# Two-layer cross-attention on one core: the sums of the second layer's softmax are formed by DMA, GpSimd and VectorE in place of TensorE

## The chip, the cores and the metric

The kernel runs on one core of a Trainium2 chip. The metric is the device time of one execution in microseconds (us). Before the change it is 2887.03 us, the median of three runs (2881.52 to 2888.2).

## What is computed

The input is a batch of four sequences, `x` (4 x 1024 x 512) and a context (4 x 1024 x 384), in f32. Two cross-attention layers follow one another; only the second is touched. Cut to what matters:

```python
# layer 0: layernorm, 16 heads of 64, softmax over 1024 keys, projection, x = x + out
# layer 1:
xn = x * rsqrt(mean(x * x) + 1e-5) * norm_w
q = rotate(xn @ wq), k = rotate(ctx @ wk)          # 16 heads of 32
q, k = q / |q|, k / |k|
attn = softmax(q @ k.T * sqrt(32), over 1024 keys)
x = x + (attn @ v) @ wout
```

Since the rows of q and k have length 1, no maximum is subtracted in layer 1: the exponentials are taken of the scores as they are, `attn @ v` is formed with the unnormalized exponentials, and the result is divided by their sum over the keys.

## The kernel before, in words

The four batches are done one after the other. For each, layer 0 is a stage of some 500 us and layer 1 one of some 240 us. The order of all instructions is the order in which the program issues them (L120, a hand-made schedule); each engine, and the SP queue that issues nearly all DMAs, works through its own list in that order and stops at an instruction until everything that it waits for is there.

**Layer 1.** Its 16 heads are done in two halves of eight heads; a half holds two groups `g` of four heads (four heads of 32 rows fill 128 partitions). The 1024 queries are cut into four parts `qb` of `WQ` = 256. A block is one `(qb, g)`, so a half has eight blocks (loop at L911). A block has four steps `kk` over the keys, 256 keys each; a half has 32 steps (one call of `Attention1.step`, L574, each), and the whole kernel has 64 blocks and 256 steps.

One step does this:

- TensorE: eight score products (L586), keys on the partitions and queries along the row.
- ScalarE: two exponentials of 128x1024 (L596) into `e`, which has two buffers that alternate with `kk`.
- TensorE: the product with v of the step before (L635), into the PSUM tile `av`.
- `self.u.fill(us)`: a share of other work ("units") that is waiting. In half 0 these are the projections and rotations of q and k for the second half and the values; in half 1 they are the first output projection of layer 1 (`po`, with weights `wo1` loaded by `wo_load`, L682, called at L892) and the start of the next batch: its loads (context rows L183, rows of x L274, weights L308), its transposes and projections.
- VectorE: the exponentials are added up over the step's two chunks of 128 keys (L605) and over the steps (L607, and L609 at the block's end) into `both`. What is left is a sum over the 128 partitions.

**The sums over the partitions** are what the change is about. In 56 blocks (`lone`), `late` (L655) multiplies `both` by a matrix of ones on TensorE (L659: four calls, eight instructions, since an f32 product is done in two passes). It is put at the third step of the next block and goes into the free half of that block's `av`. ScalarE copies `av` and the sums out together (L647, 128x512), and VectorE takes a reciprocal of 128x256 (L652) and multiplies (L653). In the last eight blocks of the kernel (the last half of the last batch) `sums` (L668) does the same with eight calls (L671) and without the addition of L609.

**Buffers.** `both`, and a tile `rest` that holds the copies of `av`, an unused quarter and the values of half 1, have two slots of the pool `big`; layer 0 uses the same slots for its regrouped exponentials. Layer 0 already regroups by DMA: L413 issues 16 DMAs from 32 partitions to 32 others for each block, 2048 in all, on SP.

**The SP queue around layer 1.** Before the first half the weights of layer 1 are loaded. The program then issues no DMA until the second half, whose first are `wo1` (L892), the next batch's weights (L308) and context rows (L183).

Of the kernel before, what the change touches and what calls it, by code (L numbers as in the profile page):

```python
# [33 lines left out]
F32 = mybir.dt.float32  # L34
# [76 lines left out]
def xattn_kernel(ctx: ExitStack, tc: tile.TileContext, a: dict, out: bass.AP):  # L111
# [444 lines left out]
    class Attention1:  # L556


        def __init__(self, b, units):
            self.b, self.u = b, units  # L560
            self.last = None
            self.av = None
            self.sums = self.quotient = None
            self.late = self.beside = None
            self.lone = False
            self.n = 0
            self.e = sb.tile([P, 2, 2, 2, 2, WQ], F32, tag="e", bufs=2, name=f"e1_{b}")
            self.both = sb.tile([P, 4, 4, WQ], F32, tag="big", bufs=2, name=f"both_{b}")
            rest = sb.tile([P, 4, 1024], F32, tag="big", bufs=2, name=f"rest_{b}")
            self.avs = rest[:, 0].rearrange("p (n c q) -> p n c q", n=2, c=2)  # L570
            v1 = rest[:, 2:].rearrange("p g (t f) -> p g t f", f=P)
            self.v1 = [v1[:, g] for g in range(2)]

        def step(self, half, g, qb, kk, kT, qT, v, o, us):  # L574
            n = f"{self.b}_{half}_{g}_{qb}_{kk}"
            self.n += kk == 0
            if kk == 1:
                self.add_up()
            if kk == 2 and self.late is not None:
                self.late(False)  # L580
            sc = [score(f"s1_{n}_{u}", (P, 2, 2, WQ)) for u in range(2)]
# [16 lines left out]
            self.finish()  # L598
            self.last = (half, g, qb, kk, v, es, o, self.n % 2, self.lone)
            self.u.fill(us)  # L600
# [5 lines left out]
            if 0 < kk < NT // 2 - 1:  # L606
                nc.vector.tensor_add(acc, acc, into)  # L607
            if kk == NT // 2 - 1 and self.lone:
                nc.vector.tensor_add(acc, acc, end)  # L609

# [15 lines left out]
        def product(self):  # L626
            half, g, qb, kk, v, es, o, par, lone = self.last
            n = f"{self.b}_{half}_{g}_{qb}"
# [13 lines left out]
            if end:  # L642
                s, av = self.avs[:, par], self.av
                if self.beside is None:
                    nc.scalar.copy(s[:, 0, :], av[:, 0, :])
                else:
                    nc.scalar.copy(s, av)  # L647
                    self.quotient = lambda f=self.beside: f(s[:, 1, :])
                    self.beside = None

                def divide(by=s[:, 1, :]):
                    nc.vector.reciprocal(by, by)  # L652
                    nc.vector.tensor_mul(o[g][:, qb * WQ : (qb + 1) * WQ], s[:, 0, :], by)  # L653

                def late(alone):  # L655
                    to = (av if alone else self.av)[:, 1, :]
                    for j in range(4):
                        rr = slice(j * HD1, (j + 1) * HD1)
                        nc.tensor.matmul(to[rr], ones, self.both[:, par, j], start=alone, stop=alone)  # L659
                    self.late = None  # L660
                    if alone:
                        nc.scalar.copy(s[:, 1, :], to)
                        self.quotient = divide
                    else:
                        self.beside = divide

# [7 lines left out]

                if lone:
                    self.late = late
                else:
                    self.sums = sums
# [78 lines left out]
    for b in range(B):  # L757
# [115 lines left out]
        for half in range(2):  # L873
# [27 lines left out]
            final = b == B - 1 and half == 1  # L901
            att1.lone = not final
            if final:
# [6 lines left out]
                ]  # L910
            for qb, g in blocks:  # L911
                for kk in range(NT // 2):
# [9 lines left out]
            kT, qT, v = kT1, qT1, att1.v1  # L922
        att1.finish()
        if att1.late is not None:
            att1.quotient()
            att1.late(True)
        att1.add_up()
# [47 lines left out]
```

## Time and profile before

| | |
|---|---|
| median of three runs | 2887.03 us |
| span of the profiled execution | 2885.9 us |
| mean granted TensorE clock | 0.996 |
| layer 1, half 0 of batch 1 (1214 to 1340 us): busy | PE 122.3, DVE 109.4, ACT 83.3, POOL 50.0 of 126 us |
| layer 1, half 1 of batch 1 (1340 to 1460 us): busy | PE 119.7, DVE 101.5, ACT 78.5, POOL 3.1 of 120 us |
| DMA engines, share busy in these two | 0.06 and 0.12 |

PE is TensorE, DVE VectorE, ACT ScalarE, POOL GpSimd, and SPq the queue of DMA issues on SyncE. The span is from the first to the last instruction; it lies 1.1 us under the median, so that times worked out from the trace can be set against the median as they are. The profile's groups give, for each line and shape, the count, the busy time in all, the mean of one, and the idle time of the engine ahead of them with what ended it.

### The profile page before, as it was taken

The numbers are of one execution on the slowest core, as the hardware profiler recorded it, in microseconds if no ns is written. First come the engines' busy times: TensorE is split into PE (matmuls) and PEld (weight loads), VectorE is DVE, ScalarE is ACT, GpSimd is POOL, SyncE is SP. The second block draws the span as 40 slices with busy tenths as digits, with TensorE's granted clock in tenths as the row PEclk, the third lists the DMA queues.
The fourth block names the chain that finished last, engine by engine and source line by source line (L and its number), as shares of the span: only waits on it lengthen the run. The fifth ranks groups of instructions, "written<-read, shape, count | busy, mean of one in ns | idle before, by whom it ended". The sixth has DMA issues, their size and how long they took to land.

```text
span 2885.9 us, 65749 instructions
## 1 busy us (share of the span) xinstructions
PE 2827.9 (98%) x26888; PEld 1420.5 (49%) x26888; DVE 2248.4 (78%) x3008; ACT 1430.1 (50%) x2276; POOL 947.8 (33%) x776
## 2 busy tenths in 40 slices
PE   8999999999999999999999999999999999999998
PEld 4444445555444445555544445455554444445543
DVE  5677786898777778589877777959987777785987
ACT  4443443666444444466643444446664444444664
POOL 2343344320134335342023433534202333353410
PEclk9999999999999999999999999999999999999999
DMA  5887776010298777501039887740105887773000
GB/s 138 183 188 176 174 170 150 22 37 25 73 207 189 180 173 174 128 22 36 26 93 205 195 184 165 178 103 22 37 26 121 203 196 184 163 173 83 2 2 31
DMA packets 177549, 348.81 MB, mean 121 GB/s; under 512 B 37600, under 2 KB 93152, under 8 KB 177248
## 3 DMA queue, kind: packets, MB, share of 16 engines
q1 hardware_dynamic: 175920, 343.96, 50.9%
q8 instruction: 212, 3.47, 0.5%
q14 instruction: 89, 0.73, 0.1%
q10 hardware_dynamic: 1328, 0.66, 0.1%
HBM read 67.64 MB, written 8.39 MB: 26 GB/s over the span
## 4 chain that ended last, share of the span: by engine, by line
PE 87%; DVE 3%; SPq 3%; DMA 2%; ACT 2%; issue 1%; POOL 1%; ACTq 0%; DVEq 0%
PE s L368 16%; PE av L429 14%; PE po L166 11%; PE s L586 9%; PE av L635 8%; PE pv L166 7%; PE pqT L166 7%; PE pkT L166 5%; PE q_p L166 4%; PE k_p L166 3%; SPq L413 2%; DMA eT<-e 1%; ACT e L596 1%; PE av L659 1%; DVE m L393 1%
## 5 line engine op out<-in xcount | busy, mean ns | idle before, releaser
L393 DVE TENSOR_REDUCE m<-s 128x1 f32<-128x1024 f32 x512 | 602.9, 1219 | 381.5 <-PE s L368 380.9
L596 ACT ACTIVATE e<-s 128x1024 f32<-128x1024 f32 x512 | 496.5, 1022 | 295.3 <-PE s L586 288.9
L399 POOL TENSOR_SCALAR raw<-raw,li 128x1024 f32<-128x1024 f32 x256 | 286.1, 1118 | 734.1 <-DVE li L398 725.6
L368 PE MATMUL s<-qk 64*128 64x512 f32 x2048 | 519.1, 616 | 3.0 <-ACT e L394 2.2
L394 ACT ACTIVATE e<-s,m 128x1024 f32<-128x1024 f32 x256 | 282.8, 1109 | 465.2 <-DVE m L393 224.3
L394 ACT ACTIVATE raw<-s,m 128x1024 f32<-128x1024 f32 x256 | 285.1, 1114 | 458.7 <-DVE m L393 458.7
L429 PE MATMUL av<-eT,v 128*64 128x256 f32 x4096 | 472.8, 384 | 12.2 <-DMA eT<-e 9.1
L399 POOL TENSOR_SCALAR e<-e,li 128x1024 f32<-128x1024 f32 x256 | 286.1, 1118 | 472.6 <-DVE li L398 240.3
L429 PEld LDWEIGHTS av<-eT,v 128*64 128x64 f32 x4096 | 288.2, 137 | 232.1 <-issue 94.8
L605 DVE TENSOR_TENSOR both<-e 128x512 f32<-128x512 f32 x512 | 342.8, 702 | 64.3 <-ACT e L596 62.2
L368 PEld LDWEIGHTS s<-qk 64*128 64x128 f32 x2048 | 184.8, 186 | 285.2 <-issue 168.8
L586 PE MATMUL s<-q,k 32*128 32x256 f32 x4096 | 308.0, 402 | 5.3 <-ACT q L505 2.7
L402 DVE STREAM_TRANSPOSE e<-raw 128x1024 f32<-128x1024 f32 x256 | 309.9, 1228 | 1.7 <-DMA eT<-e 1.7
L402 DVE STREAM_TRANSPOSE e<-e 128x1024 f32<-128x1024 f32 x256 | 310.0, 1229 | 0.2
L586 PEld LDWEIGHTS s<-q,k 32*128 32x128 f32 x4096 | 193.9, 185 | 142.5 <-ACT e L596 66.4
L166 PE MATMUL pqT<-hT,w 128*64 128x512 f32 (+1 forms) x1216 | 241.9, 597 | 2.5 <-ACT hT L250 2.5
L166 PE MATMUL po<-wo,vals 128*64 128x512 f32 x1024 | 234.6, 596 | 0.0
L166 PEld LDWEIGHTS pv<-w,cT 128*64 128x64 f32 (+1 forms) x3360 | 170.4, 132 | 41.8 <-issue 34.1
L296 DVE TENSOR_TENSOR x<-x,po 128x512 f32<-128x512 f32 x200 | 131.7, 678 | 70.4 <-PE po L166 69.7
L166 PE MATMUL pv<-w,cT 128*64 128x128 f32 (+1 forms) x3360 | 184.3, 274 | 0.9 <-ACT hT L250 0.7
L166 PE MATMUL pkT<-cT,w 128*64 128x512 f32 (+1 forms) x912 | 182.0, 597 | 0.0
L607 DVE TENSOR_TENSOR both<-both 128x1024 f32<-128x1024 f32 x128 | 159.7, 1248 | 4.4
(87 smaller groups left out, 2801.3 us busy)
## 6 DMA issues: line engine op xcount, KB each, us to landing
eT<-e SPq DMA_DIRECT2D x2048, 128.0 KB, 2.4
xr<-in_x_dram SPq DMA_DIRECT2D x32, 256.0 KB, 4.0
wo<-in_Wo_dram SPq DMA_DIRECT2D x16, 512.0 KB, 3.9
x<-in_x_dram SPq DMA_DIRECT2D x32, 256.0 KB, 5.0
out_dram<-x SPq DMA_DIRECT2D x32, 256.0 KB, 2.7
w<-in_Wq_dram SPq DMA_DIRECT2D x31, 256.0 KB, 3.3
c<-in_ctx_dram SPq DMA_DIRECT2D x32, 192.0 KB, 3.9
wkv<-in_wkv_dram SPq DMA_DIRECT2D x16, 384.0 KB, 3.3
```

Of the source, the lines that this page charges most:

```text
L166: nc.tensor.matmul(o[rr], lhsT[:, rr], rhs, start=start, stop=stop)
L368: nc.tensor.matmul(sc[j][:, kb * 512 : (kb + 1) * 512], pr["qT"][r[j], i * P : (i + 1) * P], pr["kT"][r[j], kb * 512 : (kb + 1) * 512], st ...
L393: nc.vector.tensor_reduce(m[:, j : j + 1], sc[j], AX.X, ALU.max, negate=True)
L394: nc.scalar.activation(e[j], sc[j].rearrange("p (g s) -> p g s", g=4), AF.Exp, bias=m[:, j : j + 1], accum_out=l[:, j : j + 1])
L399: nc.gpsimd.tensor_scalar(e[j], e[j], li[:, j : j + 1], HD0**-0.5, ALU.mult, ALU.mult)
L402: self.turn = [lambda j=j: nc.vector.transpose(self.e[:, :, i % BQ * 2 + j, :], e[j]) for j in range(2)]
L429: nc.tensor.matmul(av[r[j], :W].rearrange("p (t a i) -> p t a i", t=BQ, a=4), pr["v"][:, k, r[j]], eT[:, j, :, :, k * 32 : (k + 1) * 32], ...
L586: nc.tensor.matmul(sc[j // 2][:, j % 2, c, :], kT[rr, g, k * P : (k + 1) * P], qT[rr, g, qb * WQ : (qb + 1) * WQ], start=True, stop=True,)
L596: nc.scalar.activation(e, sc[u], AF.Exp, scale=float(np.sqrt(np.float32(HD1))))
L605: nc.vector.tensor_add(into[:, 2 * u : 2 * u + 2, :], es[u][:, :, 0, :], es[u][:, :, 1, :])
L607: nc.vector.tensor_add(acc, acc, into)
L635: nc.tensor.matmul(self.av[rr, 0, :], v[g][:, 2 * kk + c, rr], es[j // 2][:, j % 2, c, :], start=first and c == 0, stop=end and c == 1,)
```

## The change

In 56 blocks the ones on TensorE go. At a block's end `regroup` issues 16 DMAs on SP, each a 32x256 piece (32 KB) of `both`, so that the four quarters of the partitions lie beside one another along the row in `parts` (a free quarter of `rest`). At the last step of the next block, `over` has GpSimd add the four quarters (128x512, then 128x256). At the first step of the block after that, `done` has VectorE turn 32x32 blocks, reduce 128x256 to 128x8, take the reciprocal of 128x8, turn it back spread over 32, and multiply. The division comes a block later than it did. ScalarE copies only the 128x256 of `av`.

`way` says which block does what: "regroup" for all but the last block of half 1 in the first three batches ("one": ones on TensorE after the half's end, as at a half's end before), and in the last half of the last batch "regroup" for the first three blocks and "two" (L671's way) for the last five.

```diff
-            if kk == 2 and self.late is not None:
-                self.late(False)
...
-            if kk == NT // 2 - 1 and self.lone:
-                nc.vector.tensor_add(acc, acc, end)
+            if kk == NT // 2 - 1:
+                if self.way != "two":
+                    nc.vector.tensor_add(acc, acc, end)
+                self.over()
+                if self.way == "regroup":
+                    self.regroup(self.n % 2, g, qb, o)
+            if kk == 0:
+                self.done()
+
+        def regroup(self, par, g, qb, o):
+
+            for a in range(4):
+                for j in range(4):
+                    nc.sync.dma_start(
+                        self.parts[j * HD1 : (j + 1) * HD1, a], self.both[a * HD1 : (a + 1) * HD1, par, j]
+                    )
+            s = self.avs[:, par]
+
+            def spread():
+                t, by = self.parts, s[:, 1, :]
+                nc.gpsimd.tensor_add(t[:, :2], t[:, :2], t[:, 2:])
+                nc.gpsimd.tensor_add(by, t[:, 0], t[:, 1])
+                self.turn = turn
+
+            def turn():
+                by = s[:, 1, :]
+                l = sb.tile([P, WQ // HD1], F32, tag="l1", bufs=1, name=f"l1_{self.b}_{self.n}")
+                nc.vector.transpose(by, by)
+                nc.vector.tensor_reduce(l, by.rearrange("p (c i) -> p c i", i=HD1), AX.X, ALU.add)
+                nc.vector.reciprocal(l, l)
+                nc.vector.transpose(
+                    by.rearrange("p (c i) -> p c i", i=HD1), l.unsqueeze(2).to_broadcast([P, WQ // HD1, HD1])
+                )
+                nc.vector.tensor_mul(o[g][:, qb * WQ : (qb + 1) * WQ], s[:, 0, :], by)
+
+            self.spread = spread
+
+        def over(self):
+            if self.spread is not None:
+                self.spread()
+                self.spread = None
+
+        def done(self):
+            if self.turn is not None:
+                self.turn()
+                self.turn = None
...
-                if self.beside is None:
-                    nc.scalar.copy(s[:, 0, :], av[:, 0, :])
-                else:
-                    nc.scalar.copy(s, av)
-                    self.quotient = lambda f=self.beside: f(s[:, 1, :])
-                    self.beside = None
+                nc.scalar.copy(s[:, 0, :], av[:, 0, :])
...
-            for qb, g in blocks:
+            for i, (qb, g) in enumerate(blocks):
+                att1.way = "two" if final and i > 2 else "one" if half == 1 and i == 7 else "regroup"
...
         att1.finish()
+        att1.done()
         if att1.late is not None:
-            att1.quotient()
-            att1.late(True)
+            att1.late()
```

More of the change, by code (lines that the diff above doesn't have):

```diff
@@ L563, in __init__ @@
             self.sums = self.quotient = None
-            self.late = self.beside = None
-            self.lone = False
+            self.late = None
+            self.way = "regroup"
             self.n = 0
@@ L570, in __init__ @@
             self.avs = rest[:, 0].rearrange("p (n c q) -> p n c q", n=2, c=2)
+            self.parts = rest[:, 1].rearrange("p (a q) -> p a q", q=WQ)
+            self.spread = self.turn = None
             v1 = rest[:, 2:].rearrange("p g (t f) -> p g t f", f=P)
@@ L598, in step @@
             self.finish()
-            self.last = (half, g, qb, kk, v, es, o, self.n % 2, self.lone)
+            self.last = (half, g, qb, kk, v, es, o, self.n % 2, self.way)
             self.u.fill(us)
@@ L626, in product @@
         def product(self):
-            half, g, qb, kk, v, es, o, par, lone = self.last
+            half, g, qb, kk, v, es, o, par, way = self.last
             n = f"{self.b}_{half}_{g}_{qb}"
@@ L643, in product, with divide, late @@
                 s, av = self.avs[:, par], self.av
-                if self.beside is None:
-                    nc.scalar.copy(s[:, 0, :], av[:, 0, :])
-                else:
-                    nc.scalar.copy(s, av)
-                    self.quotient = lambda f=self.beside: f(s[:, 1, :])
-                    self.beside = None
-                def divide(by=s[:, 1, :]):
+                nc.scalar.copy(s[:, 0, :], av[:, 0, :])
+                def divide():
+                    by = s[:, 1, :]
                     nc.vector.reciprocal(by, by)
                     nc.vector.tensor_mul(o[g][:, qb * WQ : (qb + 1) * WQ], s[:, 0, :], by)
-                def late(alone):
-                    to = (av if alone else self.av)[:, 1, :]
+                def late():
+                    to = av[:, 1, :]
                     for j in range(4):
                         rr = slice(j * HD1, (j + 1) * HD1)
-                        nc.tensor.matmul(to[rr], ones, self.both[:, par, j], start=alone, stop=alone)
+                        nc.tensor.matmul(to[rr], ones, self.both[:, par, j], start=True, stop=True)
                     self.late = None
[L661 to L665, printed above, removed]
+                    nc.scalar.copy(s[:, 1, :], to)
+                    self.quotient = divide
                 def sums():
@@ L673, in sums @@
                     self.quotient = divide
-                if lone:
+                if way == "one":
                     self.late = late
-                else:
+                elif way == "two":
                     self.sums = sums
@@ L901, in xattn_kernel @@
             final = b == B - 1 and half == 1
-            att1.lone = not final
             if final:
```

## The prediction, made before the changed kernel was run

> **What bounds the kernel.** I read the busy shares first, then the groups, then the order of time around layer 1.
>
> ```profile
> PE 2827.9 (98%) x26888; PEld 1420.5 (49%) x26888; DVE 2248.4 (78%) x3008; ACT 1430.1 (50%) x2276; POOL 947.8 (33%) x776
> ```
>
> TensorE is busy nearly always, and the chain of work that ended last gives it 87%. In layer 1 it is the same: PE fills 120 of 120 us in half 1 of batch 1. So each TensorE instruction taken out there shortens the run, as long as nothing else becomes late. The nearest to that is VectorE: in the second part of half 0 of batch 0 (567 to 629 us) PE has 62.0 us busy and DVE 58.7. From the groups, shapes kept apart:
>
> ```profile
> L652 DVE RECIPROCAL rest<-rest 128x256 f32<-128x256 f32 x64 | 111.8, 1746 | 7.8 <-ACT rest L672 5.3 <-ACT rest L662 1.5 <-ACT rest L647 0.9
> L653 DVE TENSOR_TENSOR o<-rest 128x256 f32<-128x256 f32 x64 | 27.2, 425 | 2.2
> L659 PE MATMUL av<-both,ones 128*32 128x256 f32 x448 | 34.6, 380 | 2.1 <-ACT rest L647 2.1
> ```
>
> Third, TensorE in order of time (start, length, what), where one set of ones stands:
>
> ```profile
> 601.12 1.48 PE L166 MATMUL q_p<-wq,hT 128*32 128x256 f32 x24
> 602.41 0.61 PE L659 MATMUL av<-both,ones 128*32 128x256 f32 x8
> 602.96 1.15 PE L586 MATMUL s<-q,k 32*128 32x256 f32 x16
> ```
>
> From one start to the next the ones take 0.55 us; the 0.61 includes an overlap.
>
> **What is saved.** The "one" way goes from 56 blocks to 3: 53 x 0.55 = 29.2 us. The "two" way goes from 8 to 5, each 16 instructions or 1.0 us: 3.0 us. Together 32.2 us of TensorE, if TensorE remains the bound everywhere.
>
> **VectorE and GpSimd.** Per block VectorE loses 1.75 + 0.425 = 2.17 us. It gets two turns (the row of 128x1024 takes 1.23, so a quarter is 0.31 to 0.43), a reduce (0.68 at 128x512, so 0.34 to 0.41), a short reciprocal (0.12 for 128x1) and the same multiplication (0.425): 1.5 to 1.8 us. It wins some 0.4 us a block. But GpSimd gets two additions (1.27 us for 128x512 at L285, half of that for 128x256: 1.9 us), and they get in VectorE's way, as one place shows:
>
> ```profile
> 606.71 1.37 POOL L492 TENSOR_TENSOR rot<-rot,q_r 128x512 f32<-128x512 f32 x1
> 607.20 1.95 DVE L607 TENSOR_TENSOR both<-both 128x1024 f32<-128x1024 f32 x1
> ```
>
> L607 usually takes 1.23; here it took 0.72 more and ended about 1.1 us after GpSimd did. So the price per block for VectorE is between 0 (GpSimd yields) and 1.9 us. There is also a wait: the turns wait for GpSimd, in whose list they may stand behind a rotation (0.6 + 3.2 + 1.6 us, L488, L170, L492). In the changed program's order one or two of the eight blocks of half 0 have a rotation in their last step. There VectorE has 3.8 us of work before the turn, against 5.4 + 1.9 = 7.3 us on GpSimd: a wait of up to 3.5 us, with all of VectorE's next additions behind it, and behind those the exponentials, since `e` has two buffers. Where VectorE has a fifth of its time free (first part of half 0, end of half 1) this costs nothing; in the four tightest blocks of each half 0 it eats the saving. I take off 16 x 0.55 = 9 us there and 5 us for the waits: of 32 us, 18 remain. Bounds: 32 (all hidden) and -8 (all locks and waits fall on the bound).
>
> ScalarE's copy falls from 0.59 to 0.37 us; it is half idle, so I count nothing.
>
> **The queue that is moved past.** This decides it. SP's issues around layer 1 of batch 0, before the change:
>
> ```profile
> 483.85 18.28 SPq L684 DMA_DIRECT2D wo<-in_wout_dram  x2
> 562.08 0.37 SPq L308 DMA_DIRECT2D w<-in_Wk_dram  x1
> ...
> 563.64 70.44 SPq L183 DMA_DIRECT2D c<-in_ctx_dram  x8
> 640.56 1.75 SPq L274 DMA_DIRECT2D xr<-in_x_dram  x4
> ```
>
> `wo1` (L684) stands in the program at the start of half 1, yet SP, which has nothing to do in half 0, issues it at 484 to 502 us; its first user runs at 627:
>
> ```profile
> 626.54 1.23 DVE L609 TENSOR_TENSOR both<-both 128x1024 f32<-128x1024 f32 x1
> 627.19 1.90 PE L166 MATMUL po<-wo,o 128*32 128x512 f32 x16
> ```
>
> In the changed program eight groups of 16 regroup DMAs of half 0 stand ahead of `wo1`. The last of them waits for L609's sum of the eighth block, which ends at 626.54 + 1.23 = 627.8, 0.6 us after TensorE's list has come to `po` (0.6 in the other three batches too). Only then can 16 DMAs be issued, then `wo1`, then it must land; `po` and everything behind it on TensorE stand still. The program has that wait on `po`.
>
> How long are 16 issues? The nearest rows: a 2 KB load (L154) takes 0.43 us of issue, and three follow each other at 0.47; the context rows (L183) take 0.33 at the least; L413, the same form with 128 KB, 0.51 at the least, and its first 16 take 10.13 us (0.63 each) while the DMA engines are busy. For 32 KB I take 0.47: 7.5 us, bounds 5.3 and 10.1. `wout` lands 4.6 us after issue (all of L684: 3.5 to 7.1). TensorE stands still for 0.6 + 7.5 + 4.6 = 12.7 us; bounds 0.6 + 5.3 + 3.5 = 9.4 and 0.6 + 10.1 + 7.1 = 17.8.
>
> [...]
>
> After a stall TensorE is slow. Around 104 to 108 us it idles for 4.0 us, and the granted clock (last but two columns) falls to half:
>
> ```profile
> 104.00:106.00 2.00, 0.00 (x0) 0.00 (x0) 2.00 (x2) 0.00 (x0) 0.00 (x0) 1.00 0.97 195
> ...
> 108.00:110.00 2.00, 2.00 (x10) 1.37 (x12) 1.93 (x3) 1.92 (x3) 0.42 (x1) 0.50 1.06 205
> 110.00:112.00 2.00, 2.00 (x12) 1.22 (x10) 0.67 (x2) 0.38 (x2) 1.81 (x2) 0.50 1.04 199
> ```
>
> The 32 products that follow took 6.45 us, where the same number at 491 us took 3.6: 2.85 us lost for a stall (an idle of 2.15 us at 1230 us cost some 1.7). [...]
>
> So 12.7 + 2.85 = 15.5 us per batch, four times: 62 us. Bounds: 4 x (9.4 + 1.7) = 44 and 4 x (17.8 + 2.85) = 83.
>
> In three batches two more loads come late. The context rows follow `wo1` and five other issues later; they land about when TensorE comes to them: 0.5 us. The rows of x (L274) now stand behind the ninth group: sum at 642.8, 7.5 us of issues, 4 us to landing, so 11.5 us after the sum; VectorE wants them at 651.7, 8.9 us after it. It stands 1 to 3 us, of which 1 us gets through. 3 x 1.5 = 4.5 us (0 to 9).
>
> **Sum.** -18 + 62 + 4.5 = +48.5 us on 2885.9, and on the median of 2887: 2935 us. The extremes are -32 + 44 + 0 = +12 (2899) and +8 + 83 + 9 = +100 (2987).
>
> **Rivals.**
>
> - *The stall is covered, and it becomes faster.* SP would reach `wo1` soon enough, because the sum is early or the issues are short. Gain then 18 to 32 us: 2869 at my 18. For: before, 125 us lie between issue and use. Against: the sum is later than `po`'s turn in all four batches, and landing alone takes 3.5 us. The point of decision is a stall, with the clock, of 18 / 4 = 4.5 us per batch. Chance 0.04.
> - *Short issues.* At 0.1 us each the stall is 0.6 + 1.6 + 3.5 = 5.7, with 1.7 for the clock 7.4; four make 30 us against 32: 2885, no change. Against: no issue in the trace is under 0.33. Chance 0.05.
> - *VectorE becomes the bound in half 0.* The locks and waits cost all of the gain and more, and issues are nearer 0.63: stall 0.6 + 10.1 + 4.6 + 2.85 = 18 us, four times 72, plus 8 and 5: 2972. For: VectorE has 5% left there. Against: it has 0.4 us less to do a block. Chance 0.16.
> - *The forecast*, a stall of 12 to 17 us with the clock at each change of half and a part of the gain: 2905 to 2965. Chance 0.75.
>
> Range 2903 to 2972: it leaves out the two cases that end at 2885 and lower, and the upper end of the third. A measurement here can tell about 0.3% (8.7 us) from no change. Faster by more 0.04, within 0.05, slower 0.91.
>
> **What would show it.** In the changed profile: no ones but in 3 + 5 blocks; SP issuing `wo1` some 8 us after the last L610 (L609's successor) of each half 0; an idle TensorE of about 12 us before the first `po`, released by the DMA of `wo1`, four times, each followed by a clock of 0.5; regroup issues near 0.47 us; VectorE's two-input additions longer where GpSimd adds. I am wrong if `po` does not wait, if the issues take a tenth of that, or if the time goes to VectorE waiting for GpSimd in every block.

## The result, and the profile after

The changed kernel takes 3046.2 us (median of four runs, 3041.5 to 3047.6) against 2885.9 us (median of four too, 2881.5 to 2888.2) for the kernel before: a ratio of 1.056, 95% interval 1.0545 to 1.0579. It is slower by 160 us, where 48.5 were forecast and 2972 was the end of the range. The direction and the place of the largest loss were right; the sizes were not.

The page of the changed kernel: busy shares, the chain that ended last by engine and by line, and the regrouping's row among the DMA issues (count, KB each, us to landing).

```profile
PE 2859.5 (94%) x26416; PEld 1424.5 (47%) x26416; DVE 2272.4 (75%) x3179; ACT 1419.5 (47%) x2273; POOL 1084.5 (36%) x888
...
PE 63%; DVE 11%; SPq 10%; POOL 6%; DMA 5%; issue 3%; ACT 1%; POOLq 0%; DVEq 0%; ACTq 0%
...
rest<-both SPq DMA_DIRECT2D x896, 32.0 KB, 1.9
```

TensorE has 472 instructions less, as planned. But it fell from 98% to 94% of a longer span, and from 87% to 63% of the chain; SP's queue, VectorE and GpSimd have taken its place there. TensorE's busy time rose all the same, from 2828 to 2860 us, since its products took longer: the mean granted clock is 0.971 in place of 0.996, and the score products of layer 1 take 409 ns in place of 402. Who waited, for what (total us, times, longest):

```profile
POOL rest L628 <- DMA rest<-both: 243.2, 26, 14.5
...
ACT e L596 <- DVE both L605: 113.0, 38, 7.1
...
PE po L166 <- DMA wo<-in_wout_dram: 82.8, 4, 21.3
DVE rest L635 <- POOL rest L629: 63.1, 28, 5.8
...
DVE st L216 <- DMA xr<-in_x_dram: 30.9, 8, 11.1
```

The third line is the forecast stop at `wo1`, four times, but 20.7 us each in place of 12.7. The others were not in the sum, or only with small amounts; the second does not occur before the change. Of the last line, 12.6 us lie at the kernel's start, where the kernel before waits too (10.2); 18.3 are new. The stop of batch 0, taken apart, engine by engine (start, length, what, idle before it and who ended it). TensorE:

```profile
627.23 1.07 PE L679 MATMUL av<-e,v 128*32 128x256 f32 x16
649.09 3.28 PE L166 MATMUL po<-wo,o 128*32 128x512 f32 x16 [20.79 <-DMA wo<-in_wout_dram]
```

VectorE's end of the eighth block's sum; GpSimd's additions for the seventh; then SP:

```profile
629.83 1.23 DVE L610 TENSOR_TENSOR both<-both 128x1024 f32<-128x1024 f32 x1
```

```profile
633.02 1.26 POOL L628 TENSOR_TENSOR rest<-rest 128x512 f32<-128x512 f32 x1 [11.65 <-DMA rest<-both]
634.36 0.73 POOL L629 TENSOR_TENSOR rest<-rest 128x256 f32<-128x256 f32 x1
```

```profile
635.11 10.00 SPq L621 DMA_DIRECT2D rest<-both  x16
645.16 1.09 SPq L721 DMA_DIRECT2D wo<-in_wout_dram  x2
```

TensorE is free at 628.30. The sum ends at 631.06, 2.8 us later. SP doesn't begin then: there is one buffer `parts`, so the eighth group of DMAs waits until GpSimd has added up the seventh, at 635.09, 4.0 us more. Sixteen issues take 10.05 us to the issue of `wo1` (0.59 us each is the median, 0.63 from one to the next), and 3.9 us pass until `po` starts. 2.8 + 4.0 + 10.1 + 3.9 = 20.8. In the other three batches it is 1.8 to 2.8, 4.0 to 4.8, 10.1 and 4.0 to 4.1. The seventh group was itself late: issued at 621.39, 4.7 us after its sum, because the additions of the sixth stood behind a rotation in GpSimd's list until 619.28.

The clock around it (stretch, its length, then the busy times; the granted clock is last but two):

```profile
632.00:640.00 8.00, 0.00 (x0) 0.00 (x0) 0.00 (x0) 0.00 (x0) 1.99 (x2) 0.50 0.12 29
...
648.00:652.00 4.00, 2.91 (x16) 0.59 (x16) 0.00 (x0) 0.00 (x0) 0.58 (x1) 0.52 1.12 352
652.00:654.00 2.00, 2.00 (x32) 1.14 (x32) 1.56 (x3) 0.53 (x1) 0.00 (x0) 1.00 1.06 358
```

TensorE resumes at 649.09 and has its full clock at about 652; its first 16 products took 3.28 us where before they took 1.90. The clock falls as was forecast; the loss here is 1.4 us, where 2.85 were put into the sum. At the other three stops the half clock lasts 4.7 to 5.1 us after TensorE resumes, an estimated 2.3 to 2.5 us of loss.

The same one buffer carries the delay to the batch's end. From the trace of half 1 of batch 0, SP and GpSimd:

```profile
766.02 11.04 SPq L621 DMA_DIRECT2D rest<-both  x16
```

```profile
763.56 1.29 POOL L628 TENSOR_TENSOR rest<-rest 128x512 f32<-128x512 f32 x1 [12.16 <-DVE both L610]
764.93 1.06 POOL L629 TENSOR_TENSOR rest<-rest 128x256 f32<-128x256 f32 x1
778.59 1.27 POOL L628 TENSOR_TENSOR rest<-rest 128x512 f32<-128x512 f32 x1 [12.60 <-DMA rest<-both]
```

A group is issued after GpSimd's additions of the group before (end 765.99, start 766.02), takes 11 us, lands, and is added: 15.0 us from one addition to the next, about as long as a block (14.6 to 15.5 us from 703.9 on). So a lag is made up only where the blocks are slower than this loop. The row at 763.56 names VectorE and not the DMA; the group's last landing lies 0.16 us ahead of it, as at 718.87 and 733.48, so I take the landing as what ended that wait too. At the end of half 1 VectorE waits for the last of them (turn at 780.7), and layer 0 of the next batch begins late: 464.5 to 465.4 us before, 472.5 to 473.5 now.

### The profile page after: what moved, and what is told of

The parts are those of the page before. It is cut to its first block, busy times and chain, and to the rows that moved or that the text cites. A ratio compares the mean times of both kernels' runs of the same rounds, so it can differ in the third digit from the quotient of the medians.

```text
span 3045.1 us, 66474 instructions
## 1 busy us (share of the span) xinstructions
PE 2859.5 (94%) x26416; PEld 1424.5 (47%) x26416; DVE 2272.4 (75%) x3179; ACT 1419.5 (47%) x2273; POOL 1084.5 (36%) x888
## 4 chain that ended last, share of the span: by engine, by line
PE 63%; DVE 11%; SPq 10%; POOL 6%; DMA 5%; issue 3%; ACT 1%; POOLq 0%; DVEq 0%; ACTq 0%
PE s L368 15%; PE av L429 14%; PE po L166 10%; SPq L621 9%; PE pv L166 6%; PE pqT L166 6%; PE pkT L166 4%; DVE both L605 3%; PE s L586 3%; PE k_p L166 2%; POOL rest L628 2%; DMA eT<-e 2%; DMA rest<-both 2%; PE av L679 2%; DVE both L607 2%
## 5 line engine op out<-in xcount | busy, mean ns | idle before, releaser
L394 ACT ACTIVATE raw<-s,m 128x1024 f32<-128x1024 f32 x256 | 285.4, 1115 | 472.1 <-DVE m L393 471.9
L429 PE MATMUL av<-eT,v 128*64 128x256 f32 x4096 | 473.4, 384 | 10.5 <-DMA eT<-e 8.8
L605 DVE TENSOR_TENSOR both<-e 128x512 f32<-128x512 f32 x512 | 367.6, 754 | 62.8 <-ACT e L596 49.0
L586 PE MATMUL s<-q,k 32*128 32x256 f32 x4096 | 331.8, 409 | 38.7 <-ACT e L596 34.8
L586 PEld LDWEIGHTS s<-q,k 32*128 32x128 f32 x4096 | 203.8, 187 | 200.4 <-ACT e L596 134.6
L166 PE MATMUL po<-wo,o 128*32 128x512 f32 (+1 forms) x824 | 132.5, 637 | 85.7 <-DMA wo<-in_wout_dram 82.8
L628 POOL TENSOR_TENSOR rest<-rest 128x512 f32<-128x512 f32 x56 | 84.5, 1510 | 348.9 <-DMA rest<-both 243.2
```

Source lines behind the costliest of these rows:

```text
L166: nc.tensor.matmul(o[rr], lhsT[:, rr], rhs, start=start, stop=stop)
L394: nc.scalar.activation(e[j], sc[j].rearrange("p (g s) -> p g s", g=4), AF.Exp, bias=m[:, j : j + 1], accum_out=l[:, j : j + 1])
L429: nc.tensor.matmul(av[r[j], :W].rearrange("p (t a i) -> p t a i", t=BQ, a=4), pr["v"][:, k, r[j]], eT[:, j, :, :, k * 32 : (k + 1) * 32], ...
L586: nc.tensor.matmul(sc[j // 2][:, j % 2, c, :], kT[rr, g, k * P : (k + 1) * P], qT[rr, g, qb * WQ : (qb + 1) * WQ], start=True, stop=True,)
L605: nc.vector.tensor_add(into[:, 2 * u : 2 * u + 2, :], es[u][:, :, 0, :], es[u][:, :, 1, :])
L628: nc.gpsimd.tensor_add(t[:, :2], t[:, :2], t[:, 2:])
```

## The experiments

Measure of all runs: the time of the run, that of the kernel before on the same chip beside it, and the time of layer 1 in the profiled execution, summed over the four batches (988.1 us before; from the first score product of layer 1 to the first of the next layer 0, or the end). The kernel before read 2875.8 to 2889.8 us in such single runs, so a few us of a run's time say nothing; its blocks repeat to about 0.1 us (block 1 apart, which takes 19.3 to 21.4), and the last column is what is read. Block 1 alone makes it uncertain by some 5 us: its four together are 82.3 us before and 78.9 to 85.0 in the runs. Layer 0 of batch 0, which no run touches, reads 472 to 480 us. Blocks are counted from 0 in each half; where an expectation says blocks 10 and 12, both halves are counted through, and they are blocks 2 and 4 of half 1. Line numbers shift by one or a few between the variants.

| run | us | before beside it | layer 1 against before |
|---|---|---|---|
| changed kernel | 3046.2 | 2885.9 | +140.8 (and layer 0 of batches 1 to 3: +24) |
| e1_queue_only | 2974.3 | 2885.2 | +86.5 |
| e2_no_dma | 2935.9 | 2885.2 | +47.1 |
| e3_two_parts | 3050.3 | 2885.2 | +156.8 (layer 0: +7) |
| e4_wo_early | 3038.5 | 2885.2 | +127.7 (layer 0: +25) |
| e5_turns_only | 2861.5 | 2889.8 | -23.7 |
| e6_no_wait | 2911.5 | 2889.8 | +28.4 |
| e3b_two_parts | 3008.9 | 2889.8 | +119.8 |
| e7_tail_back | 2947.4 | 2889.8 | +49.3 (layer 0: +10.5) |
| e10_four_issues | 2958.3 | 2881.1 | +75.0 |
| e11_one_input | 2921.8 | 2881.1 | +33.6 |
| e9_fold | 2946.0 | 2881.1 | +65.4 |
| e9b_fold_some | 2915.3 | 2881.1 | +40.7 |
| e12_short_adds | 2864.5 | 2875.8 | -18.5 |
| e9c_later | 2890.4 | 2875.8 | +9.9 |
| e9d_later_all | 2904.4 | 2875.8 | +24.1 |
| e9e_room, 5 rounds | 2886.3 | 2885.5 | +1.1 |
| e9f_not_last, 5 rounds | 2872.7 | 2883.5 | -5.0 (layer 0: -7.5) |

Theory A, the prediction's: SP's issues ahead of `wo1` make the stop. Theory B, the rival: GpSimd's additions and the turns' waits make VectorE the bound.

**The DMAs alone (e1_queue_only).** The kernel before, with the 16 DMAs read by nobody, at the end of 53 of the 56 blocks (848 DMAs; the last half of the last batch has none):

```diff
+            if kk == NT // 2 - 1 and self.regrouped:
+                for a in range(4):
+                    for j in range(4):
+                        nc.sync.dma_start(self.parts[...], self.both[...])
```

> The kernel before, with nothing added but the 16 regroup DMAs of each of the 56 blocks; nobody reads what they bring, the sums still come from TensorE. Theory A (SP's issues: 16 of 0.63 us stand ahead of the loads of half 1): without GpSimd in the loop a group starts when the block's sum is there, so the first po of half 1 waits 0.6 + 10.1 + 4.0 = 14.7 us and 2 us go to the clock, four times 67 us, with 2 us for the rows of x in three batches: 2886 + 73 = 2959 us (2940 to 2975), blocks inside the halves as before. Theory B (GpSimd's additions hold VectorE up, issues cost little): 2886 to 2915.

A holds, and higher than its own number: 2974.3, +89. All blocks keep their times but two. Block 0 of half 1 goes from 15.6 us to between 32.4 and 33.7 (batch 3: 11.3 to 28.0), 68.7 us in all; block 2 of half 1 from 15.5 to between 20.8 and 23.2, 18.5 us in three batches. Their waits:

```profile
PE po L166 <- DMA wo<-in_wout_dram: 59.5, 4, 15.7
...
DVE st L216 <- DMA xr<-in_x_dram: 27.7, 5, 10.7
```

The first is 14.9 us a batch; 17.2 with the clock, where the forecast had 15.5. The second holds the late rows of x, but its longest wait, 10.7, is the one at the kernel's start, which stands alone before the change:

```profile
DVE st L216 <- DMA xr<-in_x_dram: 10.2, 1, 10.2
```

The other four come to 5.2 to 6.3 us in each of three batches, and the blocks lose 6 us each, forecast 1.5. Without a reader there is no loop through the buffer, so this is the price of issuing alone.

**Everything but the DMAs (e2_no_dma).** `parts` is set to ones once a batch.

```diff
-            for a in range(4):
-                for j in range(4):
-                    nc.sync.dma_start(self.parts[...], self.both[...])
```

> The changed kernel without its regroup DMAs: the quarters are set to one once a batch, so the sums and the output are not the reference's; the GpSimd additions, VectorE's turns and all order stay. Theory A: all that SP delays is gone (the stop at each change of half, the slow half 1, the late start of layer 0); what is left is the TensorE saving of 32 us less some 4 to 7 us per half 0 where the turn waits for GpSimd behind a rotation: 2860 to 2885 us. Theory B: the loss stays, over 2960 us.

2935.9, between the two: neither A nor B alone. There is a loss of 47 us in layer 1 that has nothing to do with SP, though TensorE has 32 us less to do. Some half of the blocks fall by 0.2 to 0.5 us; in half 0 block 4 goes from 14.8 to 18.4, block 5 from 15.1 to 17.2 (15.5 in batch 0) and block 7 from 14.8 to 17.3, and in half 1 block 0 from 15.6 to 19.4 (17.9 in batch 0), block 2 from 15.5 to 16.9 and block 4 from 15.4 to 19.3.

**Which part of that (e5, e6, e12, e11).** The four run without DMAs. e5 takes GpSimd's additions away and lets VectorE turn a constant; e6 keeps the additions but lets the turn not read them; e12 keeps the wait but makes the two instructions 128x8; e11 is e6 with one-input instructions.

```diff
 # e5
-                nc.gpsimd.tensor_add(t[:, :2], t[:, :2], t[:, 2:])
-                nc.gpsimd.tensor_add(by, t[:, 0], t[:, 1])
 # e6
-                nc.gpsimd.tensor_add(by, t[:, 0], t[:, 1])
+                nc.gpsimd.tensor_add(t[:, 0], t[:, 0], t[:, 1])
 # e12
+                nc.gpsimd.tensor_scalar(t[:, 0, :8], t[:, 0, :8], 1.0, 1.0, ALU.mult, ALU.mult)
+                nc.gpsimd.tensor_scalar(by[:, :8], t[:, 0, :8], 1.0, 1.0, ALU.mult, ALU.mult)
 # e11, twice
+                nc.gpsimd.tensor_scalar(t, t, 1.0, 1.0, ALU.mult, ALU.mult)
```

> The changed kernel without its regrouping DMAs and without GpSimd's additions: VectorE's five instructions a block stay and turn a constant that is set once a batch, so what is left out is the sum over keys. The run without the DMAs alone took 2935.9 us, 51 above the kernel before, though TensorE had 32 us less to do. Theory G (GpSimd's additions cost it, by holding VectorE's additions of two inputs or by making the turn wait): without them 2855 to 2890 us, and the blocks 4, 5 and 7 of half 0 come back to 14.8, 15.1 and 14.8 us from 18.4, 17.2 and 17.3. Theory V (VectorE's own added work costs it, the acc + end addition in the last step and the turns in the first): the time stays at 2915 to 2936 us and those blocks stay late.

> The same without the DMAs, GpSimd's two additions kept at their place, but their sum goes to a place that VectorE's turn does not read (it turns a constant, so the sum over keys is left out): the additions still stand beside VectorE's work, only the turn's wait for them is gone. If the wait (33.3 us of VectorE's idle time in the run without the DMAs, in front of 25 turns) is what costs, the time falls to within 10 us of the run without GpSimd's additions. If it is the additions' own time beside VectorE's additions of two inputs (these took 767 ns in place of 702 and 1351 in place of 1225), or their place in GpSimd's queue, the time stays within 10 us of 2936 us.

e5: -23.7 us in layer 1, and the late blocks are back (14.4, 14.6, 14.2). So TensorE's saving is real, and VectorE's five instructions a block cost at most the 8 us that are missing from 32. e6: with the additions beside it but no wait, +28.4: the additions alone cost 52 us. With the wait (e2) 19 more. The time, 2911.5 us, lies in neither of the ranges that were expected: the wait and the additions both count.

What the additions do shows in VectorE's rows that have no other reason to change (busy, mean ns). e5:

```profile
L606 DVE TENSOR_TENSOR both<-e 128x512 f32<-128x512 f32 x512 | 342.7, 702 | 50.7 <-ACT e L597 47.5
...
L611 DVE TENSOR_TENSOR both<-both 128x1024 f32<-128x1024 f32 x59 | 72.3, 1225 | 2.0
...
L233 DVE TENSOR_SCALAR xr<-xr,mv,rs 128x512 f32<-128x512 f32 x32 | 15.3, 543 | 2.8 <-POOL rs L170 2.8
```

and e6:

```profile
L606 DVE TENSOR_TENSOR both<-e 128x512 f32<-128x512 f32 x512 | 383.4, 782 | 49.2 <-ACT e L597 46.5
...
L611 DVE TENSOR_TENSOR both<-both 128x1024 f32<-128x1024 f32 x59 | 80.1, 1358 | 2.0
...
L233 DVE TENSOR_SCALAR xr<-xr,mv,rs 128x512 f32<-128x512 f32 x32 | 23.6, 799 | 2.8 <-POOL rs L170 2.8
```

VectorE is busy 69.8 us longer (2243.5 to 2313.3) for 145.8 us of additions on GpSimd: 0.48 us for each. And they don't come one block at a time. GpSimd in e6, batch 0, half 1:

```profile
690.77 0.19 POOL L218 TENSOR_SCALAR ve<-mv 128x4 f32<-128x4 f32 x1 [26.48 <-DVE mv L217]
691.05 1.02 POOL L170 TENSOR_TENSOR rs<-ve,nhalf 128x4 f32<-128x4 f32 x1
692.04 1.56 POOL L624 TENSOR_TENSOR rest<-rest 128x512 f32<-128x512 f32 x1
693.68 1.60 POOL L625 TENSOR_TENSOR rest<-rest 128x256 f32<-128x256 f32 x1
695.36 1.34 POOL L624 TENSOR_TENSOR rest<-rest 128x512 f32<-128x512 f32 x1
...
704.09 0.79 POOL L625 TENSOR_TENSOR rest<-rest 128x256 f32<-128x256 f32 x1
```

GpSimd's list had reached the scale of the next batch's norm, which waits 26.5 us for VectorE; behind it five pairs of additions pile up (the "..." hides six instructions) and then run in a row, 692 to 705 us. In just that time VectorE:

```profile
692.50 2.19 DVE L611 TENSOR_TENSOR both<-both 128x1024 f32<-128x1024 f32 x1
694.61 4.66 DVE L233 TENSOR_SCALAR xr<-xr,mv,rs 128x512 f32<-128x512 f32 x4
699.19 2.89 DVE L606 TENSOR_TENSOR both<-e 128x512 f32<-128x512 f32 x2
```

2.19 in place of 1.23, 4.66 where the kernel before has 1.91 for the same four, 2.89 in place of 1.29; and TensorE then stood 4.2 us. The block took 22.1 us in place of 15.4. The heap belongs to the runs without DMAs (e2 has it too, with half as many additions). In the changed kernel each group of DMAs is issued only after the additions ahead of it and takes 10 us, so that in half 1 of batch 0 the pairs lie 14.6 us apart and more, and these three rows are lengthened less (754, 1261 and 669 ns).

> The run without DMAs and without the turn's wait (2911.5 us; 2861.5 without GpSimd's additions), with GpSimd's two additions replaced by two multiplications by one of 128 x 1024 elements, with one input each, at the same place of its queue (the sum over keys is left out); from the 1.12 us that such an instruction takes in layer 0, 2.2 us a block in place of 2.6. Theory L (an addition of two inputs on GpSimd holds VectorE's instructions of two inputs while it runs, and the other way round): with one input nothing is held, and the time is 2858 to 2875 us. Theory Q (it is their place in GpSimd's queue, behind the scale of the norm that waits for VectorE for up to 27 us, that makes them run in a heap): the time stays at 2900 to 2915 us.

One input changes nothing: 147.9 us of GpSimd, 72.5 us more of VectorE, 0.49 for each, and layer 1 at +33.6. So theory L falls: it isn't the second input. The heap (Q) is there again; the time, 2921.8 us, is 7 us over Q's range.

> The run without DMAs (2935.9 us) with GpSimd's two additions replaced by two instructions of 128 x 8 elements at the same place of its queue, and the turn still waits for them (the sum over keys is left out). Theory Q (what the turn's wait costs is the place: the additions stand behind the norm's scale, which waits up to 27 us for VectorE, and VectorE stands behind the turn): the wait stays, and the time is 2880 to 2890 us, some 24 over the run with the turns alone (2861.5). Theory D (the wait is no longer than the additions themselves last, held beside VectorE): 2858 to 2868 us.

With the same place in the list and the same wait, but short instructions, layer 1 stays at -18.5: the place by itself costs 5 us more than e5, 10 if block 1 is left out of both (wait of the turn 16.4 us in all, against 33.3 in e2). So theory D (2864.5 us is in its range): in the main it is the length of GpSimd's work, beside VectorE, and the wait for it while it runs.

**The one buffer (e3_two_parts, e3b_two_parts).** A second `parts` in two rows of the rotation scratch.

```diff
-            return self.t[:, self.n % 4], self.t[:, 4 + self.n % 2], self.t[:, 6 + self.n % 2]
+            return self.t[:, self.n % 4], self.t[:, 4], self.t[:, 5]
...
+            self.two = [rest[:, 1]..., tmp.t[:, 6:]...]
```

> The changed kernel with two buffers for the quarters, used in turn; the second lies in two rows of the rotation's scratch, which gets three and one rows in place of four and two. Theory A with a loop (issues 10.1, landing 1.4, additions 2.4 us, then the next group's issues, through the one buffer): the loop is cut, a group starts at its block's sum, the stop at the change of half falls from 20.8 to 14.7 us, the start of layer 0 is no longer late (8 us in three batches), half 1 loses half of its 6 us: 3046 - 24 - 21 - 12 = 2989 us (2970 to 3005). If the issues alone count and no loop does, no change: 3046 (3035 to 3055). Theory B: no change either.

> The changed kernel with two buffers for the regrouped parts, the second in two rows of the rotation scratch, whose first tile keeps its four buffers (t2 and sq have one each here). Theory A with the loop (a block's sixteen DMAs wait for GpSimd's additions of the block before, because of the one buffer, so SP's queue never catches up): layer 0 of the batches 1 to 3 comes back from 472 to 465 us, and the time is 3010 us (3000 to 3022). If SP's issue time alone sets how late the queue is, the time stays within 6 us of 3046 us.

e3 gave the first scratch tile three buffers in place of four, and lost some 9.5 us in block 2 of each half 0 by that; it says nothing on the loop. e3b: 3008.9, 37 less than the changed kernel; layer 0 of batches 1 to 3 is back at 463.8 to 465.9, the stop at `wo1` falls from 20.7 to 17.9 us: the eighth group now begins 0.07 us after its sum, but the sum comes 2.6 to 4.2 us after TensorE is free. The loop through the buffer is shown, at 21 us in layer 1 and 23 in the layer 0 behind it, by the profiled executions; the whole runs differ by 37, since layer 0 of batch 0 reads 479.5 us in e3b and 472.1 in the changed kernel.

**The loads (e4_wo_early, e7_tail_back).** e4 issues `wo1` ahead of half 0; e7 lets the last two blocks of half 0 sum on TensorE, so that SP is free ahead of `wo1` (all of the last half of the last batch too).

```diff
 # e4
             n = 0
             if half == 0:
+                wo1 = [wo_load(a["wout"], i, f"wo1_{b}_{i}") for i in range(2)]
 # e7: the kernel before, and in it
+                att1.group = not final and i != 7 and not (half == 0 and i == 6)
...
+                if self.group:
+                    self.regroup(self.n % 2, g, qb, o)
```

> The changed kernel with the two loads of wo1 put ahead of half 0, and nothing else. Theory A: in the first three batches the next weights and context rows still stand behind the eighth group; TensorE stops two steps later at the context's transposes for nearly as long (18 to 20 us in place of 20.8), only the last batch, which has no such loads, is freed (24 us with the clock): 3046 - 31 = 3015 us (3005 to 3030). If the load of wo1 were itself what is late: four stops gone, 3046 - 96 = 2950 us.

> The regrouping in all blocks but the last two of half 0, which take their sums on TensorE as the kernel before does (and the last of half 1, as in the changed kernel); so SP has no regrouping to issue in the 15 us and more before wo1's load. Theory A (SP's issues ahead of wo1's load make the stop at the change of half): the stop of TensorE there falls from 20.8 us to under 3 us in each batch, the first block of half 1 from 38 us to 15 to 18 us, and the time is 2955 us (2940 to 2972). Theory B (the stop comes from the engines' waits and only shows at the load): the first block of half 1 stays over 30 us and the time over 3000 us.

e4 gained only 8 us and lies 8 us over A's range: the stop moved to the next thing behind the groups, the context's transposes.

```profile
PE ptc L192 <- DMA c<-in_ctx_dram: 67.9, 8, 21.2
```

Only in batch 3, which has no next batch, block 0 of half 1 came back (35.5 to 14.4 us), and the loop took a part of that again: blocks 1 to 3, which the stop had given time to catch up, go from 12.2, 12.2 and 13.0 to 15.9, 15.1 and 15.1 us, about the length of the loop, with the turn waiting 2.0 us for GpSimd in each. e7: 2947.4, as A said. No stop is left at `wo1`, block 0 of half 1 takes 16.5 us, and with the stop nearly two thirds of the loss are gone (160 to 58). What stays is as large in layer 1 as the part without DMAs (+49.3 against +47.1), though not in the same blocks: block 2 of half 1, with the late rows of x, takes 21.6 us (16.9 in e2), block 0 16.5 (19.4). In layer 0, behind the half that still regroups, another 10.5 stay.

**Fewer issues (e10_four_issues).**

```diff
-            for a in range(4):
-                for j in range(4):
-                    nc.sync.dma_start(self.parts[j * HD1 : (j + 1) * HD1, a], self.both[a * HD1 : (a + 1) * HD1, par, j])
+            for a in range(4):
+                nc.sync.dma_start(self.parts[:, a], self.both[:, par, a])
```

> The changed kernel with four DMAs a block in place of sixteen, each of 128 rows of 1 KB, so the same bytes and rows land but not regrouped (the four sums of a head are not brought together, so the sum over keys is left out). Theory A (the number of DMAs that SP issues, 0.59 us each, makes the queue late): a group takes SP some 2.5 us in place of 10, the stop at the change of half goes, layer 0 of the batches 1 to 3 is back at 464 to 466 us, and what stays is the price of the part without DMAs (2935.9 us): 2930 to 2955 us. Theory B (the rows or bytes of the DMAs set SP's time or the landing): the time stays over 3010 us.

A DMA of 128 KB takes SP 0.60 us (median), as one of 32 KB does, and as those of layer 0 did before the change (ns: least, median, most; before, changed kernel, e10):

```profile
L413 SPq DMA_DIRECT2D eT<-e x2048: 507/590/2356, 48.3 to 2615.4; - x187
```

```profile
L621 SPq DMA_DIRECT2D rest<-both x896: 507/589/1953, 515.2 to 2972.0; - x180
```

```profile
L620 SPq DMA_DIRECT2D rest<-both x224: 464/599/1629, 516.8 to 2878.9; - x112
```

The time is 2958.3, nearer to A, 3 us over its end: layer 0 is back, but of the stop 10.7 us a batch remain, though the eighth group doesn't wait for GpSimd there: VectorE's sum of the eighth block ends 3.6 to 4.2 us after TensorE is free, the group begins 0.07 us after it, four issues take 2.4 us, and 4.0 to 4.2 pass from the issue of `wo1` to `po`. The number of issues sets SP's time. When they may begin is set by the loop in the changed kernel, and by VectorE's late sum once the loop is short.

**A version without DMA and GpSimd (e9_fold, e9b_fold_some, e9c_later, e9d_later_all, e9e_room, e9f_not_last).** VectorE turns `both` in 32x32 squares and adds the columns; TensorE adds the four key groups with eight columns per call.

```diff
+                nc.vector.transpose(t, t)
+                nc.vector.tensor_reduce(l, t.rearrange("p (c i) -> p c i", i=HD1), AX.X, ALU.add)
...
-                        nc.tensor.matmul(to[rr], ones, self.both[:, par, j], start=alone, stop=alone)
+                        nc.tensor.matmul(to[rr], stack, l[:, j * C : (j + 1) * C], start=alone, stop=alone)
```

> A version without regrouping DMAs and without GpSimd: VectorE turns the block's 128 x 1024 sums in 32 x 32 squares (about 1.23 us from the row of layer 0) and adds each square's 32 columns in the next block's first step (about 1.2 us), TensorE then adds the four key groups with four multiplications of eight columns by a stacked identity in place of four of 256 columns (0.62 us a block), and VectorE takes 128 x 8 reciprocals, spreads them by a turn and multiplies. If TensorE's time is what a block costs, it falls by 0.3 to 0.5 us in each of 60 blocks: 2859 to 2870 us. But VectorE gets 1.3 us more a block, and in blocks 4 to 7 of half 0 it was busy 61.6 of 65 us before: if it becomes the bound there, these sixteen blocks take up to 1 us more each, and the time is 2875 to 2900 us.

> The same, only in the blocks where VectorE has room: the first four of half 0 and all of half 1 (but the last batch's half 1, as ever); the other blocks of half 0 as in the kernel before. If TensorE's time is what a block costs and VectorE's room there carries the 1.3 us more, 45 blocks fall by 0.3 to 0.5 us each: 2863 to 2873 us, against 2886 to 2890 us before. If the turns delay what else VectorE does in half 1 (the norm's rows of the next batch), the time is 2885 us or more.

The eight small products take 0.22 us in place of 0.61. Both were slower all the same, e9_fold by more than expected: TensorE's list now stands behind VectorE's turn. The weight load of the small products in e9_fold:

```profile
PEld av L687 <- DVE l L623: 84.4, 43, 4.1
```

> The version with the sums turned and added on VectorE, in the first two blocks of half 0 and all of half 1, with TensorE's four multiplications of eight columns moved from the next block's third step to its end, just ahead of its last attention product (the same move for the old way in the other blocks). The run before it lost its gain where TensorE stood behind VectorE's turn (2.5 us in one block). If that was all, TensorE's 0.4 us a block in 32 blocks come out: 2868 to 2878 us. If VectorE itself is too full in half 1 beside the norm's rows, the blocks 10 and 12 stay at 17 and 19 us and the time at 2885 us or more.

> The same in all blocks. If TensorE's waits were all: 2862 to 2872 us. If VectorE is the bound in the blocks 3 to 7 of half 0 (it was busy 61.6 of 65 us there before, and gets 1.3 us more a block): 2880 to 2910 us.

```diff
-            if kk == 2 and self.late is not None:
-                self.late(False)
+            if end and self.late is not None:
+                self.late(False)
```

Moved to `product`, ahead of the block's last attention product, the waits go, and in all blocks the loss falls from 65.4 to 24.1 us. In the blocks where VectorE has room the 0.3 to 0.4 us come out (blocks 2 and 3 of half 0: 14.6 to 14.3, 14.8 to 14.4). In the blocks 2 and 4 of half 1, beside the norm's rows, e9c still loses 2.3 and 1.2 us, and e9d 1.4 and 2.1 us in blocks 4 and 5 of half 0: there VectorE is too full.

> The version with the sums turned and added on VectorE and the multiplications of eight columns at the block's end, only where VectorE's turns and divisions meet neither the chains of half 0's blocks 3 to 7 nor the norm's rows in the blocks 2 and 4 of half 1: the first two blocks of half 0 and the last four of half 1, 21 blocks in all. By the blocks of the run before it (14.6 to 14.3, 14.8 to 14.4, 15.0 to 14.5, 14.7 to 14.6 and 11.0 to 10.8 us) some 1.3 us a batch: 2880 us where the kernel before takes 2885, a ratio of 0.998. If the turns delay VectorE's other work there too, the ratio is 1.000 or more.

Kept where it gained only, it comes to a ratio of 0.9997 (0.9986 to 1.0008) over five rounds: no difference. The blocks did gain, 1.0 us in half 1 and 0.7 in half 0 of a batch, but at the end of half 1 no block follows in which VectorE's turn could lie. TensorE and then layer 0's first products in e9e:

```profile
748.76 0.25 PE L687 MATMUL av<-l,stack 128*32 128x8 f32 x8 [3.07 <-DVE r L674]
748.94 3.68 PE L370 MATMUL s<-qk 64*128 64x512 f32 x8
```

TensorE stands 3.07 us, and the eight products after it take 3.68 us in place of 1.99; from the last step to layer 0 it is 8.0 us in place of 6.0. So that block too goes back to the ones:

```diff
-                att1.fold = not final and (i < 2 if half == 0 else i > 3)
+                att1.fold = not final and (i < 2 if half == 0 else 3 < i < 7)
```

> The run before it, but the last block of half 1 sums on TensorE in the old way: there no block follows, TensorE stood 3.07 us behind VectorE's turn and began the next layer 0 at half clock, so that from the last step to layer 0 it took 8.0 us in place of 6.0 in three batches, which gave back what the blocks had gained. If that was all, 1.0 us in half 1 and 0.5 to 0.7 us in half 0 come out in each batch, 5 to 7 us in all: a ratio of 0.9976 to 0.9983, and 6.0 us again from the last step to layer 0. If the gain goes elsewhere, the ratio stays at 0.9995 or more.

2872.7 against 2883.5 us, a ratio of 0.9963, 95% interval 0.9949 to 0.9977: this version is faster than both kernels, than the one before by 0.4%. From the last step to layer 0 it is 5.9 us. Layer 1 has the 5.0 us expected; the rest of the gain, over what was expected, lies in layer 0 of batches 1 and 2 (460.9 us each for 464.5 and 464.8), which in other runs with an unchanged layer 0 also reads 461 to 467: that part isn't explained.

## Why the prediction was wrong, point by point

- **TensorE's saving: 32.2 us. Right in kind, three quarters in size.** e5 has it with nothing against it but VectorE's instructions: 23.7 us in layer 1, 27 in the span.
- **"of 32 us, 18 remain": the step that failed worst.** It took 14 us off for GpSimd's additions and the waits for them. They cost 52 and 19 us in the runs without DMAs: the net is a loss of 47 us (e2), outside the bounds of 32 and -8 that the step gave. Three things were mis-set. The price was counted only in the four tightest blocks of each half 0, with the rest free because VectorE has a fifth of its time there; but without the DMAs the additions of half 1 pile up behind the norm's scale and run in a heap. VectorE's room is an average, a heap is not. (In the changed kernel the DMAs keep them apart; its blocks 4 and 5 of half 0 take 18.4 and 17.2 us, as in e2.) A single wait of up to 3.5 us was foreseen rightly (3.54 at 555.6 and at 621.4), but the waits of the turn were taken as 5 us in all, where VectorE waited 33 us in e2 and 63 in the changed kernel.
- **"For 32 KB I take 0.47: 7.5 us". Mis-sized.** 0.59 us each, 0.63 apart, 10.05 us for sixteen: the upper bound, 10.1. The row that fitted was L413, the same form, whose first sixteen took 10.13; I had put these down to busy DMA engines, and chose between the rows by size, where 32 and 128 KB make no difference (e10). L413's median over all its 2048 issues, in the same row as the least that I took, was 0.59 too. A regrouping DMA has landed 1.9 us after its issue (median); the issues of sixteen take 10.05.
- **The stop, 0.6 + 7.5 + 4.6 = 12.7 us, with the clock 15.5.** With the DMAs alone it is 14.9 and 17.2 (e1), so this term was some 10% low in all. In the changed kernel it is 20.8. What was missing is the 4.0 us (4.0 to 4.8 in the four batches) for which the eighth group waits for GpSimd's additions of the seventh: I had looked for what stands behind the DMAs, and not for what their one buffer makes them wait for. In batch 0 VectorE's sum also came 2.8 us after TensorE was free, not 0.6.
- **The clock, 2.85 us: right in kind, somewhat high** (17.2 - 14.9 = 2.3 in e1, 1.4 at the changed kernel's first stop). TensorE has its full clock 2.8 us after it resumes at the first stop, and 4.7 to 5.1 us after at the three others.
- **Late rows of x and context, 4.5 us.** 18.5 us in e1. I had let 1 of 1 to 3 us through; VectorE waited 5.2 to 6.3 us a batch, since sixteen issues of 10.05 us, not 7.5, stand ahead of these rows as well, and the block lost all of it. TensorE's waits for the context rows stay as they were (6.1 us before, 6.5 in e1).
- **Missing altogether:** the loop of 15 us through the one buffer, which keeps the lag until the batch's end and begins the next layer 0 8 us late, 24 us in three batches.
- **The sum.** In layer 1: 47 without DMAs and 86.5 for the issues are 134; measured are 140.8, and 24 in layer 0. The loop adds 44 (21 and 23, the changed kernel against e3b), and the parts overlap by 14 (e3b's 119.8 against 134); a part of this is probably the heap, which the DMAs prevent; how much of the 14 it is was not tried.
- **The rivals.** The third, VectorE as the bound in half 0, had more of the mechanism than the forecast, issues near 0.63 us and VectorE held, and 72 us for the stop (68.7 in e1), but only 8 us for VectorE and GpSimd, where the runs show 47, and no loop either. It was the nearest of the four and got 0.16.

What stays open: why GpSimd's work makes VectorE's instructions longer by half of its own time, with one input as with two. The runs show that it does, not by which part of the chip. Open too are the gain of e9f in layer 0 and the overlap of 14 us.

## What to carry to other kernels

When a change puts DMAs behind a buffer, draw the loop first: who must have read the buffer before the next group may be issued, and is the loop shorter than the work it must keep up with? Count each DMA by its issue, not by its bytes (here 0.59 us at 32 KB and 0.60 at 128 KB), and ask of each load that stands behind it in the queue when its first user comes; moving one load only shows the next one (e4: 67.9 us of waits for the context rows). Work put on an idle engine isn't free if it makes its neighbour slower while it runs (here VectorE by 0.48 us for each us on GpSimd), and an in-order list can save it up and let it go in one heap, in the fullest place (e6: five pairs of additions from 692 to 705 us). A saving of 0.4 us a block was had here, but only block by block, where the engine that takes over the work has room and nobody's list stands behind it.

## What the runs showed of the hardware that was not expected

- A DMA from SBUF to SBUF took SP's queue 0.59 to 0.60 us of issue at 32 KB and at 128 KB alike, 0.63 from one to the next; 16 of them took 10.05 us, where one has landed 1.9 us after its issue.
- 145.8 us of GpSimd's additions made VectorE's busy time 69.8 us longer; 147.9 us of its one-input multiplications 72.5 us. Instructions of one tensor input on VectorE were held too (L233: 543 ns in e5, 799 in e6).
- Eight products of eight columns (f32, four calls) took 0.22 us, against 0.61 with 256 columns.
